# Attention scores kept in their PSUM banks for a whole head: each key tile's product is added onto the scores of the tile before it, through the difference of the keys

## The chip, the cores and the metric

One core of a Trainium2 chip. The metric is the device time of one execution in microseconds, the median over runs of the same kernel. Five engines matter, each with its own queue that it works off in order: PE (the matrix unit), ACT (ScalarE), DVE (VectorE), POOL (GpSimd) and SP, which here does nothing but issue DMAs. PE writes its products into PSUM, eight banks of 512 float32 for each of 128 partitions; ACT and DVE read them there.

## What is computed

Two layers over `x` of 8 batches x 512 positions x 256 features. Layer 0 is a gated feed-forward block with a quantised hidden activation. Layer 1 is attention with 16 heads of 16 features and then a SwiGLU block, each on a normalised input with a conditioned scale and shift. The part that matters:

```python
q = split(x @ W_q.T)
k = split(x @ W_k.T)
v = split(x @ W_v.T)
attn = jax.nn.softmax(scale * jnp.einsum('bnqd,bnkd->bnqk', q, k), axis=-1)
o = jnp.einsum('bnqk,bnkd->bnqd', attn, v)
...
x = x + a_alpha * _attention(...)
return x + f_alpha * _swiglu(...)
```

All of it is float32 with a tight tolerance, so the kernel carries q and k as pairs (a rounded high part and the rest), and stacks the four products high x high, high x low, low x high and low x low along the contraction: 4 x 16 = 64 rows for a head.

## The kernel before

**Units and steps.** Four heads of one batch are a unit; there are 8 x 2 x 2 = 32 units. A unit has four steps, one for each key tile of 128 keys (`kc`), so 128 steps `s`. A step has two halves `p`, each with two heads `e` that lie in partitions 0 to 63 and 64 to 127 and run on PE at the same time, as two 64-row tiles ("rows" mode).

**One half-step** (`half_step`, L951 on) issues three pairs of products on PE: the *shift* pair (L964), which fills two fresh banks with minus the row maximum of each query (in three bf16 pieces, through the 0/1 matrix `pick`); the *score* pair (L966), which adds keys x queries onto it; and, six steps ahead (`LEAD`), the *maxima* pair (L981), the scores of a query tile against all 512 keys, from which DVE takes the row maximum (L990). ACT then takes the exponential of the 128 x 1024 scores (L997). The two banks of the scores are free as soon as the exponential has read them. In `scores`:

```python
pe.matmul(mem(sc)[:, e, :], pick[r, p, :], shifts[r, n % 2, :], start=True, stop=False)
...
pe.matmul(mem(sc)[:, e, :], tile_of(n, 1, p, e)[:, kc * P : (kc + 1) * P], tile_of(n, 0, p, e),
          start=False, stop=True)
```

**Weighing** (`weigh`, L1040): exponentials x values, four heads side by side in four 32-column tiles of PE ("columns" mode), added over the four key tiles in bank 4; one value column is all ones and gives the sum for the softmax.

**Shifts** (`shift`): once all four maxima of a unit are there, DVE splits them into three bf16 pieces (L1016 to L1019) and SP transposes them by a DMA into `shifts` (L1024).

**Fill work.** Everything else of the batches (normalisation, the projections to q, k, v, the projection out, SwiGLU, the last two batches of layer 0) is put between the steps, in columns mode through the helper `quarters` (L424); transposes on PE (L430) run in rows mode. The projections of q and k leave PSUM as a high part (ACT, L894) and a low part (DVE, L897), go to DRAM in four DMAs each (`hld`, L900) and come back in stacked form: `load_unit` fetches a unit's q and k (L941) into one slot of the pool `qk`, of which there are three.

**The order is made by a planner** (`Plan`). Each operation is recorded with an engine, a cost, a due time `at`, the values that it reads and writes, and the pools from which these take memory. `Plan.order` plays this through and writes out an order for each engine; its choices are nudged by a list of seeds, one for each 12 planned microseconds. PSUM is one arena: pairs for scores (`sc`) and maxima (`pm`) come from banks 0-1, 5-6 and 2-3, `acc` is bank 4, and `fill` takes any bank that is free, bank 7 first. When PE goes from one mode to another the planner adds a cost. What is on an engine's queue is then fixed; on the chip the engines wait for each other by semaphores.

**Stages.** Layer 0 runs for six batches (full 128 x 128 products, L759 and L844). The attention steps begin at 227 us with the last two batches of layer 0 as fill, and last until 992 us. The rest of the last batch follows: projection out (L1110) and SwiGLU (L1159, L1200).

Of the kernel before, what the change touches and what calls it, by code (L numbers as in the profile page):

```python
# [69 lines left out]
class Op:  # L70
    __slots__ = ("engine", "cost", "fn", "deps", "vals", "at", "n", "users", "waiting", "ready", "end", "mode",
                 "gate", "mark", "loads")


class Plan:
# [21 lines left out]
    SEEDS = [  # L97
        0, 113879, 348485, 0, 0, 0, 0, 970122, 465611, 117633, 514958, 684936, 0, 0, 392520, 619706, 0,
        406307, 159306, 152031, 50962, 619251, 0, 214854, 802315, 687365, 426203, 900298, 169366, 589008,
        326468, 373742, 163356, 40571, 372312, 377975, 453824, 235393, 981439, 239670, 664576, 121456, 607420,  # L100
        713770, 165919, 545339, 550234, 584580, 376387, 816114, 933188, 583712, 236932, 207243, 693401, 0,
        25712, 1290, 332463, 279154, 820328, 680833, 732325, 692139, 589552, 112060, 491359, 825570, 877525,
        578493, 757575, 407120, 609522, 396906, 160941, 214945, 701432, 182328, 573819, 10381, 208000, 219645,
    ]
# [3 lines left out]

    def op(self, engine, cost, fn, reads=(), writes=(), at=0.0, also=(), mode="full", gate=None, mark=None, loads=False):
        o = Op()  # L110
        o.loads = loads
        o.gate, o.mark = gate, mark
        o.engine, o.cost, o.fn, o.at, o.n, o.mode = engine, cost, fn, at, len(self.ops), mode
        deps = set()
        for v in reads:
            deps.update(v.writers)
            v.readers.append(o.n)
        for v in writes:
            deps.update(v.writers)
            deps.update(v.readers)  # L120
            v.writers, v.readers = [o.n], []
        deps.discard(o.n)
        o.deps = deps
        o.vals = list(dict.fromkeys([*writes, *reads, *also]))
        for v in o.vals:
            v.touch += 1
        o.users, o.waiting, o.ready, o.end = [], len(deps), 0.0, None
        for d in deps:
            self.ops[d].users.append(o.n)
        self.ops.append(o)  # L130
        return o
# [27 lines left out]
    def order(self):  # L159
# [43 lines left out]
        while events:  # L203
# [7 lines left out]
            while again:  # L211
                again = False
                for e in free:
# [68 lines left out]
                    for u in o.users:  # L282
                        w = self.ops[u]
                        w.waiting -= 1
                        late = self.LATENCY[e] * (w.engine != e or e in ("SP", "DVE"))
                        w.ready = max(w.ready, o.end + late)
                        if not w.waiting:
                            cand[w.engine].append(w)
# [26 lines left out]
def two_layers(ctx: ExitStack, tc: tile.TileContext, x, cond_t, cond_w, up_t, down_t, qkvo_t, gh_t, out_t, out_b, out):  # L315
# [11 lines left out]
    a2 = const.tile([P, 20, S], F32, name="a2")  # L327
    aq = const.tile([P, 12, S], F32R, name="aq")
    pools = {
# [14 lines left out]
        "wq": [("2", 8), ("2", 9)],  # L344
        "q": [("2", 10), ("2", 11)],
        "qt": [("2", 12), ("2", 13)],
# [14 lines left out]
    pools["wd"] = [tuple(("2", i) for i in (10, 11, 12, 13))]  # L361
    pools["qk"] = [tuple(("q", 4 * i + j) for j in range(4)) for i in range(3)]
    pools["cw"] = [(("4", 8), ("4", 9))]
    plan = Plan(pools)

    def mem(v):

        kind, i = v.slot[0]
        arena = {"b": banks, "4": a4, "2": a2, "q": aq, "al": als, "ob": obs}[kind]
        n = len(v.slot)  # L370
        return arena[:, i, :] if n == 1 else arena[:, i : i + n, :]
# [10 lines left out]
    x1 = const.tile([P, B, NT, D], F32, name="x1")  # L382
    vts = const.tile([P, 2, NT, H, 32], F32, name="vts")
    hld = dram.tile([2, NC, 2, 8, 4, DH, S], F32, name="hld")
    zd = dram.tile([2, NC, 2, P, S], F32, name="zd")
    rd = dram.tile([2, NC, 8, S], F32, name="rd")
# [27 lines left out]
    vshift = [Val(), Val()]  # L414
    vhld = [[[[Val() for _ in range(4)] for _ in range(2)] for _ in range(NC)] for _ in range(2)]
    vzd = [[Val() for _ in range(NC)] for _ in range(2)]
# [17 lines left out]
    def load_x(b, at, gate=None, n=NT):  # L434
        for k in range(0, NT, n):
            src = x[b, k * P : (k + n) * P].rearrange("(t p) d -> p t d", p=P)
            op("SP", dma(128 * n), lambda k=k, src=src: sp.dma_start(out=x1[:, b, k : k + n], in_=src),
               writes=vx1[b][k : k + n], at=at, gate=gate)

# [4 lines left out]
    load("nw", lambda: mem(V["nw"])[:C, :D], cond_w[:, :D], -95)  # L444
    load_x(0, -90, n=2)
    wup, up_v = {}, up_t.rearrange("(c p) f -> p c f", p=P)
# [22 lines left out]
    for c in range(NC):  # L469
        for s in range(2):  # L470
            load("gh", lambda c=c, s=s: gh[:, c, s], gh_t[c * P : (c + 1) * P, s * FF : (s + 1) * FF],
                 80 + 20 * c + 5 * s, dma(512), ("up", 2 + c, s))
    for k in range(2):
        load("wout", lambda k=k: wout[:, 4 * k : 4 * k + 4],
             out_t[4 * k * P : (4 * k + 4) * P].rearrange("(c p) d -> p c d", p=P), 160 + 5 * k, dma(512), ("up", 4, k))
    load("ob", lambda: ob, out_b.partition_broadcast(P), 170, gate=("up", 4, 2))

# [272 lines left out]
    def up_tile(b, t, ht, at, late=False):  # L750
# [69 lines left out]
        )  # L820
        q = Val("q")
        op(
# [24 lines left out]

        op("SP", 1.5, qtrans, reads=[q], writes=[qt], at=a8)
        op("PE", 0.9, down, reads=[qt, *wq], writes=[py], at=a14, gate=after(a14) if late else None,
# [21 lines left out]
    def project(b, at, places):  # L871
# [4 lines left out]
        )  # L876
        n = 0
        for c in range(NC):
            for s in range(2):
# [18 lines left out]

                def send(l, k, hl=hl, c=c, s=s):
                    sp.dma_start(out=hld[b % 2, c, s, :, k], in_=mem(hl)[:, l * S : (l + 1) * S])  # L900

                op("ACT", act(512), high, reads=[pp], writes=[hl], at=a)
                op("DVE", dve(512), low, reads=[pp], writes=[hl], at=a)
                for k in range(4):
                    l = (k // 2, k % 2)[s]
                    op("SP", dma(256), lambda f=send, l=l, k=k: f(l, k), reads=[hl], writes=[vhld[b % 2][c][s][k]], at=a)
                n += 1
        for u in range(NT // 2):
# [10 lines left out]
            def place_v(t, u=u, pv=pv):  # L919
                i = mem(pv)[:, t * D : (t + 1) * D].rearrange("p (h d) -> p h d", h=H)  # L920
                o = vts[:, b % 2, 2 * u + t, :, :DH]
                if t == 0:
# [11 lines left out]
    def load_unit(m, at):  # L934


        b, c, j = units[m]
        w = val["qk", m] = Val("qk")
        for s in range(2):
            def fetch(s=s):  # L940
                sp.dma_start(  # L941
                    out=mem(w)[:, 2 * s : 2 * s + 2, :].bitcast(F32),
                    in_=hld[b % 2, c, s, 4 * j : 4 * j + 4].rearrange("(p e) k d s -> (e k d) p s", e=2),
                )

            op("SP", dma(512), fetch, reads=vhld[b % 2][c][s], writes=[w], at=at)

    def tile_of(m, s, p, e):

        return mem(val["qk", m])[64 * e : 64 * e + 64, 2 * s + p, :]  # L950

    def half_step(s, p):
# [4 lines left out]
        if now is not None:  # L957
            n, kc = divmod(now, 4)
            sc = Val("sc")

            def scores():
                for e in range(2):
                    r = slice(64 * e, 64 * e + 64)
                    pe.matmul(mem(sc)[:, e, :], pick[r, p, :], shifts[r, n % 2, :], start=True, stop=False)  # L964
                for e in range(2):
                    pe.matmul(  # L966
                        mem(sc)[:, e, :], tile_of(n, 1, p, e)[:, kc * P : (kc + 1) * P], tile_of(n, 0, p, e),
                        start=False, stop=True,
                    )

            op(
                "PE", 0.455, scores, reads=[val["qk", n], vshift[n % 2], V["pick"]], writes=[sc], at=at, mode="rows",
                mark=None if p else s,
            )
        if then is not None:
# [3 lines left out]
            def maxima():  # L979
                for e in range(2):  # L980
                    pe.matmul(  # L981
                        mem(pm)[:, e, :], tile_of(m, 0, p, e)[:, qc * P : (qc + 1) * P], tile_of(m, 1, p, e),
                        start=True, stop=True,
                    )

            op("PE", 0.22, maxima, reads=[val["qk", m]], writes=[pm], at=at, mode="rows", loads=True)
        if then is not None:
# [13 lines left out]
    def shift(m):  # L1001
# [25 lines left out]

        op("SP", 1.2, send, reads=[vthird[k]], writes=[vshift[k]], at=at)

    def weigh(s):  # L1030
# [7 lines left out]
        def products():  # L1038
            for i in range(4):
                pe.matmul(  # L1040
                    mem(pa)[32 * i : 32 * i + 32, :], vts[:, b % 2, kc, 8 * c + 4 * j + i, :],
                    mem(es[i // 2])[:, (i % 2) * S : (i % 2 + 1) * S], start=kc == 0, stop=kc == NT - 1,
# [266 lines left out]
```

## Time and profile before

| what | value |
|---|---|
| median of 3 runs | 1074.0 us (1071.14 to 1075.46) |
| the profiled execution | 1073.79 us, of which span 1072.0 us |
| granted PE clock | 0.997 |
| PE busy in the span | 1053.9 us, 98% |
| DVE, ACT, POOL busy | 639.9, 516.4, 204.2 us |
| attention, 227 to 992 us (765 us): PE, DVE, ACT, POOL busy | 761.0, 485.1, 413.0, 159.8 us |
| the end, 992 to 1072 us: PE, DVE, ACT, POOL busy | 76.1, 18.7, 18.3, 27.4 us |
| DMA | 116.93 MB, queue q1 at 38.5% of the 16 engines |

A matmul's end in the trace is modelled and overlaps the start of the next, so the mean duration of one (386 ns for a shift product) is not what it adds to the stream. The chain of work that ended last gives the latter: there a run of pairs is listed with the time that each adds. In DMA issues, "landing" is not recorded by this profile; when a DMA has landed is seen only from who waited for it.

### The profile page before, as it was taken

Reading aid. Unit: us, or ns where it says so; the run is one execution under the profiler, and the core shown is the slowest. Engines: PE = TensorE matmul, PEld = TensorE weight load, DVE = VectorE, ACT = ScalarE, POOL = GpSimd, SP = SyncE. Lnnn points to the kernel's source line nnn. Section 1 sums busy time; section 2 is a strip of 40 time slices with the busy share of each in tenths; the row PEclk is TensorE's granted clock in tenths of the full one; section 3 lists DMA queues with packets and bytes.
Section 4 is the critical chain, followed back from the end, with each engine's and each line's share of the span. In section 5 each row is a group of like instructions: output and inputs, shape, how many; then the busy total and the mean of one; then the engine's idle time right before and its main releaser. Section 6 shows DMA issues by size and latency. Waiting matters only on the chain.

```text
span 1072.0 us, 22302 instructions
## 1 busy us (share of the span) xinstructions
PE 1053.9 (98%) x9400; PEld 442.8 (41%) x9400; DVE 639.9 (60%) x1044; ACT 516.4 (48%) x692; POOL 204.2 (19%) x198
## 2 busy tenths in 40 slices
PE   7999989999999999999999999999999999999998
PEld 3445444443333333433343344334433443343445
DVE  3665546777777765475568556754765575572131
ACT  3434323357667554455535553644555454536221
POOL 2100000001000322042114202311231131223342
PEclk9999999999999999999999999999999999999999
DMA  7322582215452652354246326524442643311000
GB/s 196 100 69 61 166 233 66 50 35 153 121 128 76 173 140 75 99 175 156 67 114 175 106 69 175 160 68 135 142 138 76 154 143 91 116 46 46 32 21 20
DMA packets 113827, 116.93 MB, mean 109 GB/s; under 512 B 59448, under 2 KB 69880, under 8 KB 113728
## 3 DMA queue, kind: packets, MB, share of 16 engines
q1 hardware_dynamic: 113504, 115.25, 38.5%
q8 instruction: 73, 1.20, 0.4%
q10 hardware_dynamic: 224, 0.26, 0.1%
q14 instruction: 26, 0.21, 0.1%
HBM read 56.49 MB, written 46.42 MB: 96 GB/s over the span
## 4 chain that ended last, share of the span: by engine, by line
PE 92%; DMA 4%; DVE 2%; ACT 1%; issue 1%; SPq 1%; POOL 0%; ACTq 0%; DVEq 0%; POOLq 0%
PE banks L424 41%; PE banks L759 16%; PE banks L1040 10%; PE banks L964 7%; PE banks L981 5%; PE banks L966 5%; PE banks L1159 3%; PE banks L844 2%; PE banks L1200 1%; DMA a<-a 1%; PE banks L430 1%; DMA zd<-a 1%; DVE tops L990 1%; PE banks L885 1%; ACT a L997 0%
## 5 line engine op out<-in xcount | busy, mean ns | idle before, releaser
L990 DVE TENSOR_REDUCE tops<-banks 128x2 f32<-128x1024 f32 x256 | 307.9, 1221 | 134.6 <-PE banks L981 131.6
L997 ACT ACTIVATE a<-banks 128x1024 f32<-128x1024 f32 x256 | 254.2, 1023 | 167.1 <-PE banks L966 134.3
L424 PE MATMUL banks<-a,gh 128*32 128x512 f32 x1792 | 205.3, 594 | 0.0
L759 PE MATMUL banks<-a,a 128*128 128x512 f32 x384 | 175.3, 606 | 0.3 <-ACT a L722 0.3
L966 PE MATMUL banks<-aq 64*128 64x512 f32 x512 | 145.6, 578 | 0.0
L1040 PE MATMUL banks<-a,vts 128*32 128x512 f32 x1024 | 133.9, 598 | 0.0
L1187 POOL TENSOR_TENSOR a<-a 128x512 f32<-128x512 f32 x64 | 81.9, 1279 | 265.2 <-ACT a L1183 262.2
L759 PEld LDWEIGHTS banks<-a,a 128*128 128x128 f32 x384 | 72.2, 194 | 82.2 <-issue 73.4
L424 PE MATMUL banks<-wout,a 128*32 128x256 f32 x1792 | 106.0, 381 | 0.0
L424 PEld LDWEIGHTS banks<-a,gh 128*32 128x32 f32 x1792 | 54.1, 109 | 122.0 <-issue 113.2
L964 PE MATMUL banks<-shifts,pick 64*128 64x512 bf16 x512 | 100.4, 386 | 2.1 <-DVE tops L990 1.1
L1177 DVE SCALAR_TENSOR_TENSOR a<-a,banks 128x512 f32<-128x512 f32 x64 | 43.9, 686 | 92.7 <-ACT a L1172 92.6
L981 PE MATMUL banks<-aq 64*128 64x512 f32 x512 | 93.0, 404 | 1.3 <-ACT a L997 1.3
L793 DVE SCALAR_TENSOR_TENSOR a<-banks,rstds,a 128x512 f32<-128x512 f32 x64 | 47.9, 750 | 74.9 <-PE banks L759 58.8
L766 ACT ACTIVATE a<-banks,rstds 128x512 f32<-128x512 f32 x64 | 43.4, 685 | 91.4 <-PE banks L759 84.9
L964 PEld LDWEIGHTS <-pick 64*128 64x128 bf16 x512 | 25.4, 93 | 148.4 <-issue 147.6
L424 PEld LDWEIGHTS banks<-wout,a 128*32 128x32 f32 x1792 | 55.2, 110 | 51.2 <-issue 20.1
L1172 ACT ACTIVATE a<-banks 128x512 f32<-128x512 f32 x64 | 38.3, 598 | 67.9 <-PE banks L424 50.8
L1183 ACT ACTIVATE a<-banks 128x512 f32<-128x512 f32 x64 | 38.2, 598 | 67.0 <-PE banks L424 54.9
L1131 POOL TENSOR_TENSOR x<-x,a 128x512 f32<-128x512 f32 x31 | 40.4, 1309 | 141.8 <-DVE a L1122 141.8
L424 PE MATMUL banks<-a,a 128*32 128x512 f32 x512 | 59.3, 595 | 0.0
L981 PEld LDWEIGHTS banks<-aq 64*128 64x128 f32 x512 | 48.3, 186 | 21.7 <-ACT a L997 5.8
(104 smaller groups left out, 949.7 us busy)
## 6 DMA issues: line engine op xcount, KB each, us to landing
hld<-a SPq DMA_DIRECT2D x128, 256.0 KB
aq<-hld SPq DMA_DIRECT2D x64, 512.0 KB
zd<-a SPq DMA_DIRECT2D x32, 256.0 KB
a<-zd SPq DMA_DIRECT2D x16, 256.0 KB
a<-rd SPq DMA_DIRECT2D x16, 256.0 KB
out_dram<-x SPq DMA_DIRECT2D x15, 256.0 KB
x<-in_x_dram SPq DMA_DIRECT2D x7, 512.0 KB
gh<-in_gh_t_dram SPq DMA_DIRECT2D x4, 512.0 KB
```

Source lines behind the costliest of these rows:

```text
L424: pe.matmul(o[32 * i : 32 * i + 32, :], w[:, 32 * i : 32 * i + 32], r, start=start, stop=stop)
L759: (quarters if late else pe.matmul)(mem(us[half, j]), mem(ht)[:, c * S + t * P : c * S + (t + 1) * P], mem(wup[c, 2 * half + j]), start=c ...
L766: se.activation(mem(gs[j]), mem(us[1, j]), AF.Gelu, scale=rstds[:, b, t : t + 1])
L793: lambda v=us[0, j], g=gs[j], j=j: ve.scalar_tensor_tensor(mem(h)[:, j * 512 : (j + 1) * 512], in0=mem(v), scalar=rstds[:, b, t : t + 1], ...
L964: pe.matmul(mem(sc)[:, e, :], pick[r, p, :], shifts[r, n % 2, :], start=True, stop=False)
L966: pe.matmul(mem(sc)[:, e, :], tile_of(n, 1, p, e)[:, kc * P : (kc + 1) * P], tile_of(n, 0, p, e), start=False, stop=True,)
L981: pe.matmul(mem(pm)[:, e, :], tile_of(m, 0, p, e)[:, qc * P : (qc + 1) * P], tile_of(m, 1, p, e), start=True, stop=True,)
L990: lambda: ve.tensor_reduce(tops[:, m % 2, 2 * p : 2 * p + 2, qc], mem(pm), AX.X, ALU.max, negate=True),
L997: lambda: se.activation(mem(e).rearrange("p (i s) -> p i s", i=2), mem(sc), AF.Exp, scale=0.25),
L1040: pe.matmul(mem(pa)[32 * i : 32 * i + 32, :], vts[:, b % 2, kc, 8 * c + 4 * j + i, :], mem(es[i // 2])[:, (i % 2) * S : (i % 2 + 1) * S], ...
L1177: lambda t=t, i=ps[0]: ve.scalar_tensor_tensor(mem(t), in0=mem(t), scalar=1.0, in1=mem(i), op0=ALU.add, op1=ALU.mult),
L1187: "POOL", pool(512), lambda t=t, h=hid, g=gt: gp.tensor_tensor(mem(g), mem(t), mem(h), op=ALU.mult),
```

## The change

**Scores stay in their banks.** Write S_t for the shifted scores of key tile t. Before, each tile is computed anew as shift + K_t q. After, only tile 0 is: its two banks are taken once for a head pair (`val["sc", n, p]`) and held for all four steps. For the tiles 1 to 3 PE adds (K_t - K_(t-1)) q onto the same banks, after the exponential of tile t-1 has read them. So the shift pair is issued once for a unit and half instead of four times.

**Key differences.** For each k projection (16 in all) ACT copies the keys 0 to 383, DVE subtracts them from the keys 128 to 511, ACT rounds the high part of the difference and POOL takes the rest; four more DMAs of 192 KB write them to DRAM (`hdd`), and for each unit one more DMA of 384 KB fetches them (`kd`).

**Memory.** q, k and the differences have pools of their own: three slots for q, two for k, two for the differences. To make room the values lie 17 columns apart, not 32, so that a head's 32-column weight load reaches into the next head's values; those rows of the result are not read.

**Planner.** An operation can have a `lag`, an extra latency that its users see: 1.5 for the transpose of the quantised activation, 1.0 for that of the shifts. A difference pair is planned at 0.24 instead of 0.455 and is marked `loads`. The first half of `x` is loaded ahead of the first conditioning weights, the weights of layer 1 some tens of planned microseconds earlier, and the list of seeds is another one, so the whole order of the fill work is another one too.

```diff
-    aq = const.tile([P, 12, S], F32R, name="aq")
+    aq = const.tile([P, 10, S], F32R, name="aq")
+    ad = const.tile([P, 4, S - P], F32R, name="ad")
...
-    pools["qk"] = [tuple(("q", 4 * i + j) for j in range(4)) for i in range(3)]
+    pools["q"] = [(("q", 2 * i), ("q", 2 * i + 1)) for i in range(3)]
+    pools["k"] = [(("q", 2 * i), ("q", 2 * i + 1)) for i in (3, 4)]
+    pools["kd"] = [(("d", 2 * i), ("d", 2 * i + 1)) for i in range(2)]
...
-    vts = const.tile([P, 2, NT, H, 32], F32, name="vts")
+    vts = const.tile([P, 2, NT, H * (DH + 1) + 15], F32, name="vts")
+    hdd = dram.tile([2, NC, 8, 4, DH, S - P], F32, name="hdd")
...
-    load_x(0, -90, n=2)
+    load_x(0, -96, n=2)
...
-        op("SP", 1.5, qtrans, reads=[q], writes=[qt], at=a8)
+        op("SP", 1.5, qtrans, reads=[q], writes=[qt], at=a8, lag=1.5)
...
+                    hd, m = Val("hl0" if b == 0 else "hl"), S - P
+                    def earlier(pp=pp, hd=hd):
+                        se.activation(mem(hd)[:, :m], mem(pp)[:, :m], AF.Identity)
+                    def less(pp=pp, hd=hd):
+                        ve.tensor_tensor(mem(hd)[:, m : 2 * m], mem(pp)[:, P:], mem(hd)[:, :m], op=ALU.subtract)
+                    def high_less(hd=hd):
+                        se.activation(mem(hd)[:, :m].bitcast(F32R), mem(hd)[:, m : 2 * m], AF.Identity)
+                    def low_less(hd=hd):
+                        d = mem(hd)[:, m : 2 * m]
+                        gp.tensor_tensor(d.bitcast(F32R), d, mem(hd)[:, :m], op=ALU.subtract)
+                    op("ACT", act(m), earlier, reads=[pp], writes=[hd], at=a)
+                    op("DVE", dve(m), less, reads=[pp], writes=[hd], at=a)
+                    op("ACT", act(m), high_less, writes=[hd], at=a)
+                    op("POOL", pool(m), low_less, writes=[hd], at=a)
+                    send(2, hd, m, a)
...
-            sc = Val("sc")
+            if kc == 0:
+                val["sc", n, p] = Val("sc")
+            sc = val["sc", n, p]
             def scores():
-                for e in range(2):
+                for e in range(2 if kc == 0 else 0):
                     r = slice(64 * e, 64 * e + 64)
                     pe.matmul(mem(sc)[:, e, :], pick[r, p, :], shifts[r, n % 2, :], start=True, stop=False)
                 for e in range(2):
+                    k = tile_of(n, "kd", p, e)[:, (kc - 1) * P : kc * P] if kc else tile_of(n, "k", p, e)[:, :P]
                     pe.matmul(
-                        mem(sc)[:, e, :], tile_of(n, 1, p, e)[:, kc * P : (kc + 1) * P], tile_of(n, 0, p, e),
-                        start=False, stop=True,
+                        mem(sc)[:, e, :], k, tile_of(n, "q", p, e), start=False, stop=True, skip_group_check=kc > 0,
                     )
...
-        op("SP", 1.2, send, reads=[vthird[k]], writes=[vshift[k]], at=at)
+        op("SP", 1.2, send, reads=[vthird[k]], writes=[vshift[k]], at=at, lag=1.0)
...
+                h = (8 * c + 4 * j + i) * (DH + 1)
-                    mem(pa)[32 * i : 32 * i + 32, :], vts[:, b % 2, kc, 8 * c + 4 * j + i, :],
+                    mem(pa)[32 * i : 32 * i + 32, :], vts[:, b % 2, kc, h : h + 32],
```

## The prediction

> **What bounds the kernel now.** I read the page first: shares of busy time, then the chain that ended last.
>
> ```profile
> PE 1053.9 (98%) x9400; PEld 442.8 (41%) x9400; DVE 639.9 (60%) x1044; ACT 516.4 (48%) x692; POOL 204.2 (19%) x198
> PE 92%; DMA 4%; DVE 2%; ACT 1%; issue 1%; SPq 1%; POOL 0%; ACTq 0%; DVEq 0%; POOLq 0%
> ```
>
> PE is busy all through and the chain is PE. A busy PE proves little by itself, since ends of matmuls are modelled; so I looked at who makes PE wait, in the waits of PE alone:
>
> ```profile
> PE banks L844 <- DMA a<-a: 4.5, 2, 4.3
> PE banks L512 <- DMA a<-in_cond_w_dram: 3.9, 1, 3.9
> PE banks L430 <- DMA x<-in_x_dram: 1.6, 1, 1.6
> PE banks L981 <- ACT a L997: 1.3, 2, 0.8
> ```
>
> Columns are total us, times, longest. PE hardly waits; in the 765 us of attention it is busy for 761. The kernel is bound by the sum of what PE streams, so a product that is taken away counts in full, unless it brings a new wait. What a pair adds to the stream is read from the chain in order of time (start, us, what), in the middle of the attention:
>
> ```profile
> 502.98 0.32 PE banks L964 x2
> 503.31 0.23 PE banks L966 x2
> 503.54 0.23 PE banks L964 x2
> ...
> 507.73 0.47 PE banks L981 x4
> ...
> 528.74 0.86 PE banks L1040 x8
> 529.60 0.67 PE banks L981 x4
> 530.27 0.49 PE banks L430 x16
> 530.75 0.99 PE banks L1040 x8
> ```
>
> **What the change takes from PE.** A pair of 64-row products adds 0.23 us inside a run of rows-mode work, shift (503.54), score (503.31) and maxima (507.73, two pairs in 0.47) alike. In the built order of the changed kernel PE has 5492 matmuls instead of 5876: 384 fewer, all of them shift products, nothing else gone or added. That is 192 pairs x 0.23 = 44.2 us less.
>
> **What it puts back on PE.** Changing mode costs. A rows run that starts with a shift pays 0.32 - 0.23 = 0.09 us (502.98); one that starts with maxima pays 0.67 - 0.47 = 0.20 (529.60 against 507.73); the return to columns 0.99 - 0.86 = 0.13 (530.75 against 528.74). A start with transposes I take at 0.14 (0.63 against 0.49, the dearest and the cheapest L430 x16 in the chain of the attention). Why 0.09 and 0.20 is in the weight loads, which nothing hides at a run's start:
>
> ```profile
> L966 PEld LDWEIGHTS banks<-aq 64*128 64x128 f32 x512 | 51.3, 197 | 0.6 <-issue 0.6
> L981 PEld LDWEIGHTS banks<-aq 64*128 64x128 f32 x512 | 48.3, 186 | 21.7 <-ACT a L997 5.8 <-issue 5.1 <-ACT a L634 0.8
> L964 PEld LDWEIGHTS <-pick 64*128 64x128 bf16 x512 | 25.4, 93 | 148.4 <-issue 147.6 <-DMA hld<-a 0.4
> ```
>
> A bf16 `pick` loads in 93 ns, keys or queries in 186 to 197: 0.10 us more, which is the 0.11 between the starts. I counted the starts in both built orders between the first shift and the last score. Before: 175 with a shift, 12 with maxima, 1 with transposes = 15.8 + 2.4 + 0.1 = 18.3 us. After: 47 with a shift, 95 with maxima, 54 with scores, 5 with transposes = 4.2 + 149 x 0.20 + 0.7 = 34.7 us. So +16.4, and 12 more returns to columns (199 against 187), +1.6. No run of before starts with a score, so that price is bounded: 0.09 if its load were hidden after all, 0.27 as for the dearest usual start of a single maxima pair (0.50); I take 0.20, by the equal load. Over 54 starts the ends are -5.9 and +3.8. **PE's stream: -44.2 + 16.4 + 1.6 = -26.2 us.**
>
> The Trainium skill, "TensorE: Matmul & The Clock Gate", section "LDWEIGHTS (loading the stationary operand)", has the load depend on the number of columns alone, about 107 ns for 128, whatever the type. By it all starts would cost alike and the stream would come to about -43 us (an estimate from that page); the rows 93 and 197 above disagree with it, and I follow them.
>
> **New waits: the banks.** A pair of banks is now held for four steps, so of the eight banks four hold scores and one the weighed values. The next product onto them must wait for the exponential. What that takes, when nothing covers it:
>
> ```profile
> 244.87 0.25 PE banks L966 x2
> ...
> 245.14 1.03 ACT a L997
> ...
> 246.22 0.39 PE banks L964 x2
> ```
>
> From 245.10, the pair's place in the stream, to 246.22: 1.12 us. For maxima the reduction takes its place:
>
> ```profile
> L990 DVE TENSOR_REDUCE tops<-banks 128x2 f32<-128x1024 f32 x256 | 307.9, 1221 | 134.6 <-PE banks L981 131.6
> ```
>
> 1.22 + 0.1 = 1.34 with the same margins. Against these I set the PE work that the built order puts between the last product into a bank and the next onto it, priced by the pieces above. For the 192 in-place additions it is at least 0.58, at the tenth percentile 1.77, in the middle 3.1 us: weighing and fill products stand between. What is missing, summed over scores and maxima: 1.1 us after, 1.0 before. If every reader stood behind another 0.6 us operation of its engine (ACT's 128 x 512 take 598 ns): 10.3 after, 4.8 before, so +5.5; behind a further reduction (1.22): 51.7 against 34.6, +17.1. The real attention of before is 765 us where its order priced in the same way makes 756, 4.6 us of the difference a DMA; so the readers queue somewhat, less than 0.6 each. I take **+3**, ends 0.1 and 17.1.
>
> The Trainium skill, "PSUM — Partial Sum Buffer", section "Summary: rules for kernel authors", speaks against such a change: evacuate promptly, since PSUM is tight. It gives no price, and the gaps in the order leave the rule little to bite on.
>
> **Keys.** With two slots for k instead of three for both, a unit's k can be fetched only when the unit two before has made its first scores. From there to its first maxima the built order has 5.26 us of PE work at the least, 9.3 in the middle (30 units). In before's trace the second fetch of a unit was issued 6.1 us ahead of its first maxima at the least (659.4, 665.5) and PE never waited for it. Landing in 5.5 us leaves 0.5 us missing over all units, in 6.5 us 3.9. I take **+1**, ends 0 and 3.9. The differences are needed 23 us or more after their slot is free: nothing.
>
> **Shifts.** From a unit's last maxima to its first shift at least 8.0 us of PE work (before: 6.6, with no wait for the DMA). Needed: the reduction 1.22, four small DVE operations (265 + 244 + 231 + 221 ns = 0.96), the issue 1.24, and a landing of 3.9 (`rec<-zd` in the chain) = 7.3: nothing. With the slowest transpose, 6.5, five units miss 6.0 in all. I take 0, ends 0 and 6.0.
>
> **Work beside.** ACT: 32 x about 0.5 us (128x256 is 385 ns, 128x512 598) = 16 us; DVE 16 x 0.56 = 9; POOL 16 x 1.0 = 16 (756 ns for 256, 1279 for 512). They lie beside PE, with 352, 280 and 605 us free in the attention; without cover they would add 2.6 us to each of 16 chains from keys to DRAM, 41 us. They hold a fill bank a little longer, which the counted order already holds. SP issues 96 DMAs more, at 0.4 to 2.0 us each (the fetches' shortest and longest), some 60 us; each is passed by the shift transposes, the fetches and the softmax sums queued behind it, and a fetch that waits for PE holds these up. The bounds for keys and shifts above contain that. Bytes go from 117 to 142 MB, q1's share from 38 to about 47%.
>
> **Planner details.** The `lag` asks for more room behind the transposes for which PE waited 4.5 us: ends -4.5 and 0, I take **-2**. The earlier half of `x`: PE waited 1.6 us for it; the conditioning weights now come one issue (0.6) later: ends -1.6 and +0.6, taken as 0.
>
> **Sum.** -26.2 + 3 + 1 - 2 = -24.2 us against the profiled execution's own 1073.79 (0.2 under the median of the runs shown): 1049.6, so **1050 us**. Between the first shift and the last score I expect some 741 us instead of 765; the 80 us of the end stay.
>
> **Rivals.** *Starts are free*: the weight loads of the 149 starts are pulled ahead, each costs 0.09. Then -44.2 + 1.6 - 0.2 = -42.8, 1031 us. For it: PE's loads overlap inside a run. Against: eleven starts with maxima in before's chain, none under 0.19. 6%. *Late keys, no change*: landing takes 8.5 us, as `zd<-a` once did (7.74 after its issue), because more is in flight. Missing then 20.5 us: 1073.8 - 26.2 + 3 + 20.5 - 2 = 1069 us. Against: a fetch seen to land within 6.1 in the middle of writes to `hld`. 6%. *Slower: the in-place chain*. Product, exponential and next product on the same banks follow each other with no second buffer; if ACT or DVE is late, PE's fixed order stands with everything behind the waiting pair. Each fully bare addition costs 1.12 us; from 24 bare ones of 192 the gain is gone, and with one in four, 48, it is 54 us: 1073.8 - 27.2 + 54 = 1101. For it: the waits that before's chain has on L997 at all. Against: gaps of 3.1 us in the middle and an ACT that is idle 46% of the attention. 7%. That the pairs were never on the bound is excluded by the chain, where each stands with its 0.23.
>
> **Range and chances.** All low ends together give 1036. Upwards, the bank waits at their upper end add 14 and a late unit or two 3: 1067. 81% inside 1037 to 1067. A measurement of this kernel can tell 0.5%, 5.4 us, from no change. Faster: the forecast and the first rival, 87%; same: 6%; slower: 7%.
>
> **What would show it.** The shift group should have 128 products and some 25 us instead of 100.4; pieces of the chain that start with scores should cost about 0.43 for the first pair; the waits of PE for the exponential and the reduction should stay under 10 us in sum, those for DMAs under 5. The forecast is wrong if PE's busy time falls while these waits grow beyond 20 us, or if a run's start is nearer 0.09.

## The result and the profile after

| | before | after |
|---|---|---|
| median of 17 runs each | 1072.4 us (1069.2 to 1075.9) | 1066.7 us (1062.8 to 1073.0) |
| after / before, 95% interval | | 0.9951 [0.9933, 0.9969] |
| span of the profiled execution | 1072.0 us | 1065.6 us |

5.7 us faster where 24 were forecast, just inside the range's upper end and near the 0.5% that a measurement can tell from no change. The page of the changed kernel: shares of busy time, queue q1, the chain by engine.

```profile
PE 1031.6 (97%) x9016; PEld 427.0 (40%) x9016; DVE 636.9 (60%) x1060; ACT 523.9 (49%) x722; POOL 219.8 (21%) x214
...
q1 hardware_dynamic: 130912, 140.42, 47.0%
...
PE 82%; DMA 9%; DVE 4%; ACT 2%; issue 2%; POOL 1%; SPq 0%; ACTq 0%; DVEq 0%
```

PE is busy 22.3 us less, yet the span fell by 6.4. The chain tells where the rest is: PE has 82% of it instead of 92%, DMA 9% instead of 4%, DVE 4% instead of 2%. PE still does almost all the work, but its pauses are now on the path. PE's waits in after, the longest five (columns as in the prediction: total us, times, longest):

```profile
PE banks L848 <- DMA a<-a: 6.7, 3, 3.6
PE banks L1020 <- DVE tops L1029: 5.3, 7, 1.6
PE banks L1002 <- DMA shifts<-thirds: 4.6, 4, 1.7
PE banks L434 <- DMA x<-in_x_dram: 3.7, 1, 3.7
PE banks L1005 <- ACT a L1036: 2.8, 3, 1.7
```

All listed waits together are 30.0 us, where before had 14.2: for DMAs 16.3 instead of 10.0, for the reduction 5.3 instead of 1.1, for the exponential 3.4 instead of 2.0.

The groups of the products concerned, shapes kept apart (L1002 shift, L1005 scores, L1020 maxima; the 384 with `ad` are the difference products):

```profile
L1020 PE MATMUL banks<-aq 64*128 64x512 f32 x512 | 103.3, 440 | 7.5 <-DVE tops L1029 5.3 <-issue 1.8 <-ACT a L1036 0.4
L1005 PE MATMUL banks<-aq,ad 64*128 64x512 f32 x384 | 76.2, 429 | 2.9 <-ACT a L1036 2.8
...
L1002 PE MATMUL banks<-shifts,pick 64*128 64x512 bf16 x128 | 25.6, 386 | 6.1 <-DMA shifts<-thirds 4.6 <-DVE a L1218 0.5 <-DVE a L1163 0.4
```

128 shift products in 25.6 us, as worked out. Idle time ahead of them has three releasers: the reduction, the exponential and the transposes of the shifts. And the price that no run of before could show, a rows run that starts with scores, in the chain in order of time:

```profile
541.57 1.00 PE banks L428 x16
542.57 0.43 PE banks L1005 x2
543.00 0.23 PE banks L1020 x2
543.23 0.23 PE banks L1005 x2
```

0.43 at the start against 0.23 inside: 0.20.

**An account of stream and waits.** I cut the built order of PE's products at each change of mode, took from the trace when each such run begins, and set the time to the next run's beginning against the sum of its products at the prediction's prices. What is left over is counted as waiting; it also holds pauses too short for the list above and what PE loses while its granted clock is halved (a mean of 0.995 in after and 0.997 in before: at most 5.3 and 3.2 us of the spans). The prices hold: the median left over is -0.002 us for the 54 score starts, -0.002 for the 95 maxima starts, -0.003 for the 47 shift starts of after. Us, in the profiled executions:

| kernel | PE's stream, whole | waits ahead of the first shift | waits behind it | all waits |
|---|---|---|---|---|
| before | 1037.5 | 16.6 | 10.6 | 27.2 |
| after | 1010.9 | 17.3 | 30.2 | 47.5 |

So the stream fell by 26.6 (forecast: 26.2) and the waits rose by 20.3. Behind the first shift 25 runs of after lose more than 0.3 us, 25.1 us together; in before 9 did, 5.8. Three of them, as the chain of after shows them in order of time:

```profile
457.74 5.16 DMA als<-ald
462.90 0.07 issue
462.97 0.73 POOL obs L1138
463.70 0.97 POOL a L933
464.67 1.25 POOL x L1172
465.92 0.02 issue
465.95 1.85 DVE a L601 x4
467.80 1.15 DVE tops L1029
468.94 0.04 issue
468.99 0.50 PE banks L1020 x2
...
585.55 5.59 DMA rec<-zd
591.14 0.02 issue
591.16 0.35 DVE rec L1115
591.51 1.09 DVE tops L1029
592.61 0.04 issue
592.65 0.97 PE banks L1020 x6
...
696.29 5.48 DMA shifts<-thirds
701.77 0.05 issue
701.82 0.39 PE banks L1002 x2
```

The third is simple: a shift transpose lands 5.48 us after its issue and PE stands in front of the shift product. The first two only look like waits for DVE. PE's wait is put down to the reduction L1029, but the reduction had stood on DVE's queue behind an operation whose input came by DMA, `rec<-zd` 5.59 us or `als<-ald` 5.16 us after its issue. (In the first a part of the change's own work, POOL's L933 for a key difference, adds 0.97 us.) The page lists no landings for this kernel, but the trace has the semaphore records of the DMA queues, from which the landing of each can be read. Of the 88 transfers behind 215 us on which other engines hang (32 shift transposes, 48 for the softmax sums, 8 `als`; 24 of them write 256 KB each), 11 took more than 5 us to land in before and 28 in after. The median shift transpose went from 3.0 to 4.4 us, while the 16 KB `rec<-zd` stayed at 2.2 in the median.

**Theory:** the 25 MB of key differences, which the prediction priced at nothing, make other transfers land late, and a PE whose covering work has shrunk meets this, and the readers of held banks, as waits. **Rivals:** the readers alone; the added transfers' number on SP's queue; the added work on ACT, DVE and POOL.

### The profile page after: what moved, and what is told of

Its sections match the earlier page's. It is cut to its first block, busy times and chain, and to the rows that moved or that the text cites. A ratio compares the mean times of both kernels' runs of the same rounds, so it can differ in the third digit from the quotient of the medians.

```text
span 1065.6 us, 21733 instructions
## 1 busy us (share of the span) xinstructions
PE 1031.6 (97%) x9016; PEld 427.0 (40%) x9016; DVE 636.9 (60%) x1060; ACT 523.9 (49%) x722; POOL 219.8 (21%) x214
## 4 chain that ended last, share of the span: by engine, by line
PE 82%; DMA 9%; DVE 4%; ACT 2%; issue 2%; POOL 1%; SPq 0%; ACTq 0%; DVEq 0%
PE banks L428 36%; PE banks L763 16%; PE banks L1081 9%; PE banks L1020 6%; PE banks L1005 6%; PE banks L1200 3%; PE banks L848 2%; DMA shifts<-thirds 2%; DVE tops L1029 2%; PE banks L1002 1%; DMA rec<-zd 1%; DMA zd<-a 1%; DMA a<-a 1%; DMA als<-ald 1%; PE banks L1241 1%
## 5 line engine op out<-in xcount | busy, mean ns | idle before, releaser
L1029 DVE TENSOR_REDUCE tops<-banks 128x2 f32<-128x1024 f32 x256 | 308.7, 1222 | 148.3 <-PE banks L1020 140.7
L1020 PE MATMUL banks<-aq 64*128 64x512 f32 x512 | 103.3, 440 | 7.5 <-DVE tops L1029 5.3
L1020 PEld LDWEIGHTS banks<-aq 64*128 64x128 f32 x512 | 45.5, 185 | 86.2 <-DVE tops L1029 22.1
L1005 PE MATMUL banks<-aq,ad 64*128 64x512 f32 x384 | 76.2, 429 | 2.9 <-ACT a L1036 2.8
L428 PE MATMUL banks<-qkvo,a 128*32 128x256 f32 x896 | 55.7, 386 | 1.5 <-POOL a L1126 1.5
L428 PE MATMUL banks<-a,qkvo 128*32 128x512 f32 x448 | 56.0, 598 | 0.0
```

Of the source, the lines that this page charges most:

```text
L428: pe.matmul(o[32 * i : 32 * i + 32, :], w[:, 32 * i : 32 * i + 32], r, start=start, stop=stop)
L1005: pe.matmul(mem(sc)[:, e, :], k, tile_of(n, "q", p, e), start=False, stop=True, skip_group_check=kc > 0,)
L1020: pe.matmul(mem(pm)[:, e, :], tile_of(m, "q", p, e)[:, qc * P : (qc + 1) * P], tile_of(m, "k", p, e), start=True, stop=True,)
L1029: lambda: ve.tensor_reduce(tops[:, m % 2, 2 * p : 2 * p + 2, qc], mem(pm), AX.X, ALU.max, negate=True),
```

## Experiments

Times are medians, ratios go against runs of before on the same chip.

**1. The shift pairs alone, in before's order.** A shift pair is issued only for the first key tile; no differences, nothing else moved.

```diff
-                for e in range(2):
+                for e in range(2 if kc == 0 else 0):
                     pe.matmul(mem(sc)[:, e, :], pick[r, p, :], ...
...
-                        start=False, stop=True,
+                        start=kc > 0, stop=True,
```

> The kernel before, in its own order, with the shift products of the key tiles 1 to 3 left out (those scores are not shifted) and nothing put in their place: no held banks, no key differences, no DMAs. If PE's stream is the bound and only its content counts: 192 pairs x 0.23 = 44.2 us less, 14 us back because some 130 of 175 starts with a shift become starts with scores (0.11 each): about -30, 1043 us against 1073. Rival, that PE is only one of several bounds and others take over as soon as it is relieved: 1058 us or more.

1052.8 us, 0.9815 [0.9794, 0.9835]: between the two. The stream fell by 30.6, all waits rose from 27.2 to 37.3. Where products go and the order stays, about a third of the gain comes back as waits with no new byte moved and no bank held longer. The weight loads show who is waited for (a load's idle time lies partly beside PE's products, so it is not time lost by PE). In before the load of `pick` stood ahead of that of L966, which waited for nothing; now

```profile
L966 PEld LDWEIGHTS banks<-aq 64*128 64x128 f32 x512 | 47.4, 187 | 101.6 <-issue 39.9 <-DVE tops L990 19.6 <-ACT a L997 8.2
```

The shift pairs had also been cover for the readers of PSUM.

**2. The change without the transfers of differences** (`ad` is filled once; all products and the four operations behind each projection stay).

```diff
-                    lambda l=l, k=k, o=o: sp.dma_start(out=o[:, k], in_=mem(hl)[:, l * m : (l + 1) * m]),
+                    (lambda: None) if s == 2 else lambda l=l, k=k, o=o: sp.dma_start(...),
...
+                if s == 2:
+                    return
```

> The changed kernel in its own order, without the 64 DMAs that write the key differences and the 32 that fetch them (the differences are zeros, so the scores of key tiles 1 to 3 are wrong). Theory, that the gain is lost in waits for the held banks and for reductions and exponentials that come late: 2 to 5 us less than the changed kernel (ratio to before 0.991 to 0.994). Rival, that the added 25 MB make all landings late and the waits follow from that: at least 10 us less (0.986 or lower).

1053.3 us, 0.9819 [0.9786, 0.9853]: 13 us less than after. The transfers cost them.

**3 and 4. Half the readers' work.** The reduction, or the exponential, reads 256 of its 512 columns.

```diff
-  ve.tensor_reduce(tops[...], mem(pm), AX.X, ALU.max, negate=True)
+  ve.tensor_reduce(tops[...], mem(pm)[:, :, : S // 2], AX.X, ALU.max, negate=True)
```

> The changed kernel in its own order, where DVE takes the row maximum over half of the keys (256 of 512) of each maxima pair: each reduction shorter by about 0.5 us, 135 us of DVE gone. Theory, that about 9 us of PE's new waits are for reductions that come late: 7 to 10 us less than the changed kernel, ratio to before about 0.987. Rival, that the waits come from the held score banks or from DMAs: within 3 us of the changed kernel.

> The changed kernel in its own order, where ACT takes the exponential of half of the queries (256 of 512) of each score pair: each shorter by about 0.4 us, 110 us of ACT gone. Theory, that some 8 us of PE's new waits are for exponentials on held banks, a part of them after loads of the activation table and after a late shift: 4 to 7 us less than the changed kernel, ratio about 0.990. Rival, that the in-place chain costs nothing: within 2 us of the changed kernel.

1063.9 us, 0.9915 [0.9885, 0.9944], and 1067.0 us, 0.9935 [0.9912, 0.9958]. Halving the reduction brings some 3 to 4 us, with an interval that overlaps that of after; halving the exponential nothing that can be told. Neither reader's own length, one at a time, is the cause. Both halved together were not run with the transfers in place.

**5 and 6. Both kernels with an empty list of seeds**, so that the planner's own rules make the order:

```diff
-    SEEDS = [...]
+    SEEDS = []
```

> The kernel before with an empty list of seeds, so the planner's order is not nudged. Says, with its partner, what the change is worth where neither order was chosen. If the loss lies in how well each order was chosen: this one and the changed kernel without seeds should differ by about the stream's 26 us. If the loss belongs to the change itself (more and later DMAs, held banks): by 10 us or less. The time of this one is not forecast closer than 1085 to 1115.

> The changed kernel with an empty list of seeds. Theory that the loss belongs to the change itself: within 10 us of the partner without seeds, on either side. Rival, that the changed kernel's chosen order is merely a poor draw: 20 us or more below the partner.

1101.1 us, 1.0269 [1.0254, 1.0284], and 1117.1 us, 1.0416 [1.0396, 1.0436]. In plain orders the change is 16 us slower than the kernel without it, beyond the theory's 10 and far from the rival's 20 below. Its stream is only 20.7 us shorter (231 rows runs instead of 205), and all waits are 86.5 instead of 50.9. PE's longest waits for the exponential and the reduction, without the change and then with it:

```profile
PE banks L957 <- ACT a L990: 5.6, 7, 0.9
PE banks L957 <- DVE tops L983: 4.6, 5, 1.3
...
PE banks L998 <- ACT a L1029: 8.9, 11, 1.9
PE banks L1013 <- DVE tops L1022: 8.3, 10, 1.6
PE banks L995 <- DVE tops L1022: 5.2, 6, 1.6
```

Over all lines PE waits 10.4 us for the exponential without the change and 9.5 with it, and 7.5 and 18.0 us for the reduction. So the waits for the exponential, by which the in-place chain would show, did not grow; those for the reduction did. Another large part is the clock: the granted clock of the profiled execution is 0.978 with the change and 1.000 without, and 0.022 of 1115 us is 25 us at most. The prediction's slower rival is therefore not shown by this pair.

**7. All the transfers, a sixteenth of the bytes.** Each of the 96 carries 24 of the 384 columns.

```diff
-                    lambda l=l, k=k, o=o: sp.dma_start(out=o[:, k], in_=...),
+                    lambda l=l, k=k, o=o: sp.dma_start(out=o[:, k, :, : m if s < 2 else 24], in_=...),
...
+                n = 24 if s == 2 else S
```

> The changed kernel in its own order with all of its DMAs, but those of the key differences carry 24 of 384 columns (the rest of the differences are zeros, so scores are wrong). Leaving these DMAs out gave 13 us less than the changed kernel. If their bytes make other landings late: nearly the same gain, ratio to before 0.980 to 0.985. If it is their number (the issue on SP, the eight DMAs in flight, the 128 or 256 rows of each): within 4 us of the changed kernel, 0.991 to 0.995.

1053.1 us, 0.9823 [0.9802, 0.9844]: the same as with no transfers at all. It is the bytes and not the issues. All waits fall from 47.5 to 32.1, by 5.4 ahead of the first shift and by 10.0 behind it. Of the 88 transfers 6 took over 5 us instead of 28. PE's waits in the attention, where after has 4.6 for `shifts<-thirds` and 5.3 for the reduction:

```profile
PE banks L1022 <- DVE tops L1031: 3.0, 5, 1.0
PE banks L1007 <- ACT a L1038: 2.2, 3, 1.1
...
PE banks L1004 <- DMA shifts<-thirds: 0.5, 1, 0.5
```

**8. No transfers of differences and half the readers' work**, 2, 3 and 4 together.

> The changed kernel in its own order without the DMAs of the differences and with both readers halved: row maxima over half of the keys, exponentials of half of the queries (so maxima, scores and weights are wrong). Alone they gave 13, 4 and 1 us (the last two hardly clear of noise). If what is left of the waits is for readers of held banks: the stream alone, -26 us to before and no more waits than there, 1046 us, ratio 0.973 to 0.978. If it is for other things (shifts, fills, transposes): 0.980 or more.

1042.2 us, 0.9727 [0.9711, 0.9743]. All waits are 22.2, below those of before. So what is left over before's waits once the bytes are gone goes with the readers: 11 us in time between 2 and 8, 9.9 us of waits between 7 and 8. With the transfers in place halving the reduction was worth 3 (run 3) and halving the exponential nothing; but there only one reader was halved at a time, so how far the two causes overlap is not shown. The added work on ACT, DVE and POOL was not taken out by itself; it stands in this run too, whose waits are below before's.

**9. The same traffic on the kernel before.** After each send of keys a second one of 384 columns, after each fetch of a unit's keys a second one, which here writes to DRAM.

```diff
+                    if s == 1:
+                        sp.dma_start(out=hdd[b % 2, c, :, k], in_=mem(hl)[:, l * S : l * S + S - P])
...
+                if s == 1:
+                    sp.dma_start(out=ad[m % 32], in_=hdd[b % 2, c, 4 * j : 4 * j + 4].rearrange(...))
```

> The kernel before, its products and its order of instructions untouched, with the change's traffic put on top: after each of the four transfers that send a head pair's keys out, one more that sends the first 384 of their 512 columns, and after each fetch of a unit's keys one more that reads these columns back and lays them into a DRAM tile that nobody reads. That is the same 25 MB and the same 96 issues on SP's queue that the key differences bring (there the fetch goes to SBUF). Theory (the bytes in flight make other landings late, in any kernel): the shift transposes, the q and k fetches and the denominators land later, PE's waits rise by some 5 to 12 us, time 1077 to 1085 with the kernel before at 1072. Rival (before's longer products cover the later landings, and only the changed kernel is short of cover): at most 3 us more, 1072 to 1075, though the landings are later.

1105.0 us, 1.0284 [1.026, 1.0308], 31 us more: beyond both. Waits rose by 6.2 ahead of the first shift and 25.5 behind it. So a longer stream doesn't cover late landings; but the transfers also stood where no plan had put them, which left two causes.

**10. The same, with 24 of 384 columns each**, is the run that separates them (the edit is that of 9 with `:24`).

> The kernel before with the same 96 additional transfers as in the run that put the change's traffic on it (1105), in the same places, but each carries 24 of the 384 columns, so some 1.6 MB instead of 25. That run was 31 us slower where 5 to 12 were expected; open is whether the bytes or the issues in places that no plan had room for cost this. Theory (bytes): most of it goes, 1073 to 1082. Rival (issues: some 0.8 us each on SP's queue, four in a row ahead of the fetches and shift transposes behind them): 1095 to 1106.

1076.9 us, 1.0044 [1.0028, 1.0059]. Of the 31 us some 26 are bytes and 5 are issues. One place in both chains, first with the bytes:

```profile
780.60 5.82 DMA als<-ald
...
788.46 1.26 DVE a L599
...
789.94 1.15 DVE tops L996
791.09 0.04 issue
791.13 0.61 PE banks L970 x2
```

and with short transfers:

```profile
761.43 3.96 DMA als<-ald
765.46 0.73 POOL obs L1103
766.19 1.25 POOL x L1137
767.46 1.27 DVE a L599
768.95 1.15 DVE tops L996
770.14 0.39 PE banks L970 x2
```

The chain is that of after at 457.74, without the key difference: `als`, two POOL operations, DVE's square, the reduction behind it, PE. The landing differs, 5.82 against 3.96; the operations behind it take as long in both.

**11 and 12. Differences made on the chip.** If the bytes are the price, the differences shouldn't travel. POOL subtracts the fetched k tile from itself; the transfers of differences and the four operations behind each projection go. The order is that of after.

```diff
+                if qc == 1 and p == 0:
+                    k = mem(val["k", m]).bitcast(F32)
+                    gp.tensor_tensor(mem(val["kd", m]), k[:, :, P:], k[:, :, : S - P], op=ALU.subtract)
```

> The changed kernel in its own order of instructions, with the key differences made on the chip instead of sent through DRAM: POOL subtracts the fetched, stacked k tile from itself, shifted by one key tile (128 x 768 elements, once a unit, issued after the unit's third maxima pair), into the tile that the fetch filled. The 64 + 32 transfers of differences and the two ACT, one DVE and one POOL operations behind each k projection are gone. The high and the low part of k are subtracted separately and rounded once more, so the low part of a difference's rounding is not kept. Theory (25 MB in flight cost 13 us; PE's products and the late readers stay): as without the difference transfers, 1050 to 1056, PE's waits in the attention 19 to 24 us. Rival (32 operations of some 2 us on POOL, which also makes the residual stream for the transposes and products of the fill work, come in its way and stand where the landings stood): 1060 to 1068, with PE waiting for POOL's tiles for over 5 us.

1057.6 us, 0.9863 [0.9842, 0.9883], between the two. The place was poorly chosen, as the groups of POOL show:

```profile
L1027 POOL TENSOR_TENSOR ad<-aq 128x768 fp32r<-128x768 f32 x32 | 59.1, 1849 | 69.9 <-PE banks L1006 57.2 <-issue 12.7
```

Read from the right: 57.2 us of standing for the products of the unit two before, which still read the tile, then 59.1 us of work. The next run issues it one step later (`qc == 2`).

> The kernel with the differences made by POOL, with one thing changed: the subtraction is issued after the unit's fifth maxima pair instead of its third, one step later. In the run before, POOL stood 57.2 us in all in front of these 32 subtractions, for the products of the unit two before that still read the tile to be overwritten, and with it the normalisation of the weighed values that PE's projection out waits for (3.1 us of PE's waits on POOL's tiles, 1.3 on the differences). Theory: POOL no longer stands there, these 4 us go and some of the late readers' waits with them; 1050 to 1055, below the 1057.6. Rival (the wait is paid elsewhere: the waits of PE for POOL are too small a part of the attention's 27 us): 1056 to 1060.

```profile
L1027 POOL TENSOR_TENSOR ad<-aq 128x768 fp32r<-128x768 f32 x32 | 59.8, 1869 | 29.6 <-PE banks L1006 26.5 <-issue 3.1
```

1053.8 us, 0.9828 [0.981, 0.9847]: half of the standing is gone, and the time is that of the runs without the bytes. This kernel is 13 us faster than the change and 18 faster than before. It leaves out the low part of a difference's rounding; what that does to the scores is not shown here. The profiled execution took 1060.1 us, so no waits of PE are read from it.

## Why the prediction was wrong

**The failed step is "Work beside".** It counted the bytes, "117 to 142 MB, q1's share from 38 to about 47%" (47.0 came), and let them cost nothing but what the bounds for keys and shifts held. These bounds took landings one by one, from single instances in a kernel without this traffic. What happened is that many of the transfers on which other engines hang landed later, 28 of 88 over 5 us instead of 11. Runs 2 and 7 put the price at 13 to 14 us; between after and run 7 the waits differ by 15.4, 5.4 ahead of the first shift and 10.0 behind it.

**The bank waits were mis-sized, inside their bounds.** +3 was taken, 0.1 and 17.1 were the ends. With the bytes gone (run 7) the waits behind the first shift are 20.2 against before's 10.6, 9.6 more. Halving both readers takes 9.9 away again, some of which before has too: its all waits, 27.2, are above the 22.2 of run 8. The step compared how much was missing if each reader stood behind 0.6 us, and read from before's real order that they "queue somewhat, less than 0.6 each". Run 1 shows what this missed: with 384 products fewer the same readers get the same work done in less PE time. The cover is PE's own stream, and the change cuts it. One reading of the step was wrong as well: of the 9 us between the real 765 and the priced 756 it put 4.6 down to a DMA, the piece `a<-a` of the chain at 235.03. PE had other products then; in the 765 us it waited 0.2 us for that DMA:

```profile
PE banks L844 <- DMA a<-a: 0.2, 1, 0.2
```

So more of the 9 us than the step allowed is not a DMA's, and its "less than 0.6 each" had less support. (Its 1.22 + 0.1 is 1.32, not 1.34; nothing here hangs on that.)

**Right:** PE's stream, -26.6 for -26.2, with the 0.20 for score starts that was taken unseen; the loads of a bf16 `pick` (93 ns) and of keys (186 to 196) still lie 0.1 us apart, as its reason would have it. *Starts are free* is excluded by 542.57. **Keys:** +1 taken; PE never waits for `aq<-hld` in after. **Shifts:** 0 taken with an upper end of 6.0; PE waits 4.6 for them, and 0.5 in run 7, so with the bytes the term lay near its upper end. **Late keys, no change** named the right kind of cause, more in flight, at one transfer that had room. **The lag and the earlier x:** -2 taken; the waits ahead of the first shift rose by 0.7. With short transfers they are 11.9 against before's 16.6, so these edits, with the new order around them, bring 4.7, and the bytes take 5.4 back; the edits were not run alone. **The in-place chain** is shown by no run: in front of the 384 difference products PE idles 2.8 us for the exponential in after, and in the plain orders its waits for the exponential don't grow. Of the prediction's signs, that for the exponential and the reduction held (8.7 us of PE's waits, under 10), and that for DMAs did not (16.3, not under 5). Together they are 25.0, beyond the 20 that were to show a wrong forecast, while PE's busy time fell.

**The sum as measured:** -26.6 stream; +15.4 waits that go with the bytes; +4.9 for the rest of the rise, 9.6 behind the first shift less 4.7 ahead of it. Together -6.3; the spans differ by -6.4.

What stays open: whether more bytes make other transfers late by way of the shared engines of q1 or of the memory was not separated, and whether an order planned with the real landings would win back part of the waits was not tried.

## What to carry to other kernels

Where one engine is busy 97% of the span, work taken from it also takes the cover from everything that is timed by it; price the gain as stream saved minus a recount of the waits with landings later than those seen. Price added DMA bytes by what hangs on the other transfers beside them, not by the mean share of the queues, and test it by keeping the number of transfers and cutting their length. A wait that the profile puts down to an engine's operation is followed back along that engine's queue: what stood in front may have been waiting for a DMA.

## What the runs showed of the hardware

**Late landings in crowded stretches.** q1's transfers took 47.0% of the 16 engines' span in after, 44.2% in run 9, and 39.3% in run 10. Of the 88 transfers 28, 21 and 13 took over 5 us there. The mean hides where they were late: by the trace's packet records the engines of after were busy 84% of the time while the late ones were under way, and 47% while the others were; in before it was 79% and 41%. The shift transpose for which PE stood at 316.0 was under way from 308.44 to 315.95. A stretch of 8 us that holds most of this, and the whole attention (columns: us, then busy us and number of instructions of PE, its weight loads, DVE, ACT and POOL, then the granted PE clock, the DMA share and GB/s):

```profile
310.00:318.00 8.00, 6.30 (x52) 2.03 (x48) 5.54 (x6) 1.99 (x3) 0.00 (x0) 1.00 0.98 169
...
227.00:992.00 765.00, 747.06 (x7766) 282.86 (x7768) 482.12 (x756) 423.66 (x542) 175.20 (x158) 1.00 0.52 147
```

The share is 0.98 there and 0.52 on the whole.

**The clock falls after short pauses.** In after PE stood 1.0 us ahead of 316.0, for a shift transpose, and 1.75 us ahead of 319.06, for an exponential. The stretch behind, columns as above:

```profile
318.00:326.00 8.00, 6.94 (x66) 3.28 (x69) 3.57 (x7) 3.97 (x4) 0.00 (x0) 0.57 0.22 66
```

The granted clock is halved for 6.8 us from 318.5 on, and a score start takes 0.79 and 0.72 us instead of 0.43 there; this cost some 3 us on top of the pauses. The Trainium skill, "TensorE: Matmul & The Clock Gate", section "Why this matters for your kernels", asks for no idle gaps over about 3 us. Here the clock fell with two gaps of 1.0 and 1.75 us within 4 us; in the same execution a gap of 3.6 us that ended at 159.9 was not followed by such a stretch, and one of 2.2 us that ended at 168.3 was, for 3.4 us. Run 5 had gaps of 1.35 and 1.32 us within 3.3 us (ending at 231.9 and 233.7) and no such stretch. So neither the longest gap nor a pair of them tells by itself. Before had one such window, 6.8 us long, during its wait for the transposes at 156 us. In all these traces the halved stretches between two full ones last 3.4 us or two or three times that.

The waits of the account hold this loss too. The mean granted clock was 0.978 in run 6 and 1.000 in run 5, 0.989 in run 9 and 0.998 in run 10; times the span that is an estimate of at most 25 and 10 us of these pairs' differences. So a part of what a pause costs is paid at half clock behind it.
